# A layernorm, RWKV and mixture-of-experts kernel: raw x into the shared expert, zero copies behind the scatters, and another order of the work

## The chip, the cores and the metric

The kernel runs on one core of a Trainium2 chip. A core has five engines that run side by side, each through its own list of instructions in order: TensorE (PE, matmuls and transposes), VectorE (DVE), ScalarE (ACT), GpSimd (POOL) and SyncE (SP, which here only issues transfers). The metric is the device time of one execution in microseconds, and lower is better.

## The reference

x is 4 x 1024 tokens of 256 channels. The output is x + s * silu(f), where xn is the layernorm of x without weights, and s and f are two branches over xn:

```
xn = (x - mean(x)) / sqrt(var(x) + 1e-5)

s:  xt = layernorm(xn) * ln_w + ln_b ; prev = xt of the token before (0 at the first)
    K = (xt*mk + prev*(1-mk)) @ Wk.T ; V and R likewise ; R = sigmoid(R)
    S_t = S_(t-1) * decay + K_t      (a scan over the 1024 tokens of a sequence)
    s = xn + (R * ((S*first + K) * V)) @ Wo.T

f:  scores = sigmoid(xn @ router.T)      (8 experts in 2 groups of 4)
    the better group, then the top 2 experts of it, by scores + bias ; weights normed over the 2
    routed = sum over the 2 experts of weight * (silu(xn @ Wg) * (xn @ Wu)) @ Wd
    f = routed + (silu(xn @ sg) * (xn @ su)) @ sd    (the shared expert, for every token)
```

Each expert maps 256 to 128 channels and back. Everything is in float32.

## The kernel before

The 4096 tokens are 8 groups g of 512 (4 tiles of 128 tokens), and two routing batches b of 4 groups each. All of x stays in SBUF, with two more columns per token for its two routing weights. The work is cut into units, small functions, and a list written out by hand, ORDER (L25), calls them one by one. TensorE, VectorE and ScalarE run exactly in this order. The transfers that SP issues and the instructions of POOL that the list speaks of are chained too (`follow`), so that these two queues also go in the order of the list.

For a group: `moments` takes mean and variance of each tile (bn_stats, bn_aggr on VectorE), `root` and `invert` make rstd from them (ScalarE and VectorE), and `scale` (L369 to L373) writes (x - mean) * rstd over x, on VectorE or POOL as its last argument says. `turn_xn` transposes the scaled tiles to channels by tokens. `shared_in` (L869) multiplies them with one weight tile that holds the shared gate, the shared up, the router and a column of ones, so that one product per tile gives the shared expert's two halves, the router's logits and the sum over channels. `shared_turn` transposes the product of gate and up for the second half, which `shared_out` does much later. `norm2` makes rstd and offset of the second layernorm, `norm2_out` applies them on ScalarE (its result is xt), `turn_xt` transposes that. `mix` makes the three token shifted mixes, `gate`, `recur` and `value` do the products with Wr, Wk and Wv and the scan, `project_out` that with Wo.

For a routing batch: `choose`, `pick` (twice), `rank_pairs` and `place` are a chain of small operations on VectorE, with two matmuls in place, that ends in idx, a row for each token in a DRAM buffer xs. The two experts of a token make one of 19 pairs, and every pair has a region of its own in xs. `weigh` writes the two weights into the two further columns of x. `send` scatters the tokens into xs: 16 indirect transfers a batch, issued by POOL (L577), with an idle memset behind every other one (L587). `plan` and `slots` lay 128-token tiles over the filled regions.

Tiles are worked off in twos, u = 0 to 17: 4 pairs of tiles after the first batch, from whole tiles of its tokens, and 14 after the second. `tile_load` reads the rows from xs (SP, L729) once the batch's scatters have landed. `tile_turn` transposes, `tile_in` multiplies with gate and up of the two experts (the expert numbers come into registers of TensorE first), `tile_back` transposes, and `tile_out` multiplies with down, and SP writes the result to ys. After the second batch, the last tile of each of the 19 regions may end in rows that nothing was written to. So `slots` (1) also issues 19 transfers on SP (L672, "xs<-none") that put zeros behind the filled rows of each region, and the tiles of the last stage wait for them as well as for the scatters. `backs` finds where a token's result lies, `fetch` gathers it (POOL), `shared_out` and `final` add and multiply, `store` adds x and writes the output; for the last group `ready` and `finish` do the same in another order, with four writes of 128 tokens issued by SP. `over` handles inputs whose tiles are more than the 18 pairs; it isn't taken here.

`hold` is 6 transposes of a constant into a spare PSUM tile; there are 12 of them, before the first real work and around it. Transposed tiles go through 2 PSUM buffers (ps_tr), products through 4 (ps_mm), results of the down products through 2 (ps_dn).

Of the kernel before, what the change touches and what calls it, by code (L numbers as in the profile page):

```python
# [25 lines left out]
    ("moments", 0, 0), ("moments", 0, 1), ("moments", 0, 2), ("hold", 7, 6), ("moments", 0, 3), ("root", 0, 0, 1),  # L26
    ("hold", 9, 6), ("root", 0, 1, 2), ("root", 0, 2, 3), ("load_x", 4), ("hold", 8, 6), ("invert", 0, 0, 1),
    ("root", 0, 3, 4), ("invert", 0, 2, 3), ("invert", 0, 1, 2), ("invert", 0, 3, 4), ("scale", 0, 0, 0),
    ("load_x", 5), ("scale", 0, 3, 0), ("load_x", 6), ("scale", 0, 2, 0), ("scale", 0, 1, 0), ("hold", 4, 6),
    ("moments", 1, 0), ("hold", 3, 6), ("hold", 1, 6), ("hold", 10, 6), ("moments", 1, 1), ("moments", 1, 2),  # L30
    ("moments", 1, 3), ("root", 1, 0, 4), ("hold", 2, 6), ("moments", 2, 0), ("turn_xn", 0, 0), ("invert", 1, 0, 4),
    ("moments", 2, 1), ("moments", 3, 0), ("scale", 1, 0, 0), ("scale", 1, 2, 0), ("turn_xn", 0, 1), ("rates",),
    ("scale", 1, 1, 0), ("hold", 6, 6), ("hold", 11, 6), ("hold", 0, 6), ("moments", 2, 2), ("moments", 2, 3),
    ("moments", 3, 1), ("hold", 5, 6), ("root", 2, 0, 4), ("moments", 3, 2), ("moments", 3, 3), ("invert", 2, 0, 4),
    ("load_x", 7), ("root", 3, 0, 4), ("invert", 3, 0, 4), ("scale", 1, 3, 1), ("scale", 3, 1, 0),
    ("scale", 2, 0, 0), ("scale", 3, 0, 0), ("scale", 3, 2, 0), ("turn_xn", 1, 0), ("scale", 2, 3, 0),
    ("scale", 2, 1, 0), ("turn_xn", 1, 1), ("final_load", 0, 0), ("shared_in", 0, 0), ("moments", 4, 0),
    ("shared_in", 0, 1), ("moments", 4, 1), ("scale", 3, 3, 1), ("scale", 2, 2, 1), ("turn_xn", 3, 0),
    ("moments", 4, 2), ("moments", 4, 3), ("turn_xn", 3, 1), ("shared_in", 1, 0), ("moments", 6, 0),
    ("moments", 6, 1), ("moments", 6, 2), ("shared_turn", 0), ("shared_in", 1, 1), ("turn_xn", 2, 0), ("blank",),  # L40
    ("turn_xn", 2, 1), ("moments", 7, 0), ("moments", 7, 1), ("final_load", 1, 1), ("moments", 7, 2),
    ("moments", 7, 3), ("shared_in", 3, 0), ("root", 4, 0, 4), ("moments", 6, 3), ("root", 7, 0, 4),
    ("root", 6, 0, 4), ("norm2", 0, 2), ("invert", 4, 0, 4), ("invert", 7, 0, 4), ("scale", 4, 1, 0),
    ("moments", 5, 0), ("shared_in", 3, 1), ("shared_turn", 1), ("scale", 4, 2, 1), ("scale", 7, 3, 0),
    ("scale", 4, 0, 1), ("scale", 7, 2, 0), ("scale", 4, 3, 1), ("moments", 5, 1), ("load_experts",),
    ("invert", 6, 0, 4), ("shared_in", 2, 0), ("moments", 5, 2), ("load_squares",), ("scale", 6, 3, 1),
    ("shared_in", 2, 1), ("moments", 5, 3), ("scale", 6, 1, 1), ("choose", 0), ("scale", 6, 0, 1),
    ("turn_xn", 4, 0), ("turn_xn", 4, 1), ("root", 5, 0, 4), ("shared_turn", 2), ("scale", 6, 2, 1),
    ("norm2", 2, 2), ("pick", 0, 0), ("pick", 0, 1), ("shared_turn", 3), ("shared_in", 4, 0), ("turn_xn", 6, 0),
    ("turn_xn", 6, 1), ("weigh", 0), ("shared_in", 4, 1), ("scale", 7, 1, 1), ("scale", 7, 0, 1),  # L50
    ("invert", 5, 0, 4), ("turn_xn", 7, 0), ("turn_xn", 7, 1), ("rank_pairs", 0), ("norm2_out", 0),
    ("shared_in", 6, 0), ("scale", 5, 1, 1), ("shared_turn", 4), ("shared_in", 7, 0), ("norm2_out", 1),
    ("place", 0), ("turn_xt", 0, 0), ("scale", 5, 0, 0), ("plan", 0), ("scale", 5, 3, 1), ("shared_in", 6, 1),
    ("turn_xt", 0, 1), ("mix", 0, 2), ("scale", 5, 2, 1), ("turn_xn", 5, 0), ("shared_in", 7, 1), ("turn_xn", 5, 1),
    ("mix", 0, 0), ("mix", 0, 1), ("gate", 0), ("send", 0, 0), ("shared_turn", 6), ("turn_xt", 1, 0),
    ("recur", 0, 0), ("recur", 0, 1), ("turn_xt", 1, 1), ("slots", 0), ("send", 0, 1), ("shared_in", 5, 0),
    ("send", 0, 2), ("mix", 1, 2), ("shared_in", 5, 1), ("value", 0, 0, 0), ("choose", 1), ("send", 0, 3),
    ("shared_turn", 7), ("shared_turn", 5), ("norm2_out", 2), ("tile_load", 0), ("value", 0, 1, 0), ("pick", 1, 0),
    ("tile_load", 1), ("pick", 1, 1), ("gate", 1), ("turn_xt", 2, 0), ("turn_xt", 2, 1), ("tile_load", 2),
    ("tile_load", 3), ("rank_pairs", 1), ("project_out", 0, 1), ("project_out", 0, 0), ("tile_turn", 0),  # L60
    ("norm2_out", 3), ("place", 1), ("weigh", 1), ("tile_turn", 1), ("tile_in", 0, 0), ("tile_in", 0, 1),
    ("tile_turn", 2), ("plan", 1), ("mix", 1, 0), ("tile_in", 1, 0), ("send", 1, 0), ("send", 1, 1),
    ("tile_in", 1, 1), ("tile_back", 0), ("tile_in", 2, 0), ("tile_turn", 3), ("slots", 1), ("tile_in", 2, 1),
    ("mix", 1, 1), ("tile_back", 1), ("send", 1, 2), ("mix", 2, 2), ("send", 1, 3), ("tile_out", 0),
    ("turn_xt", 3, 0), ("tile_in", 3, 0), ("turn_xt", 3, 1), ("tile_in", 3, 1), ("mix", 2, 0), ("tile_back", 2),
    ("tile_load", 4), ("tile_load", 5), ("tile_out", 1), ("norm2", 4, 2), ("tile_back", 3), ("recur", 1, 0),
    ("norm2_out", 4), ("value", 1, 0, 1), ("tile_load", 6), ("recur", 1, 1), ("value", 1, 1, 0), ("mix", 2, 1),
    ("gate", 2), ("turn_xt", 4, 0), ("turn_xt", 4, 1), ("tile_load", 7), ("tile_out", 2), ("tile_turn", 4),
    ("tile_out", 3), ("norm2", 6, 2), ("tile_turn", 5), ("tile_in", 4, 0), ("tile_in", 4, 1), ("tile_turn", 6),
    ("backs", 0), ("tile_in", 5, 0), ("tile_back", 4), ("tile_in", 5, 1), ("norm2_out", 5), ("tile_load", 8),  # L70
    ("tile_turn", 7), ("tile_in", 6, 0), ("tile_back", 5), ("tile_in", 6, 1), ("tile_load", 9), ("tile_turn", 8),
    ("tile_out", 4), ("tile_back", 6), ("mix", 3, 0), ("tile_in", 7, 0), ("tile_in", 7, 1), ("backs", 1),
    ("mix", 3, 2), ("tile_load", 10), ("tile_turn", 9), ("tile_out", 5), ("tile_back", 7), ("tile_load", 11),
    ("tile_in", 8, 0), ("tile_in", 8, 1), ("tile_turn", 10), ("tile_out", 6), ("tile_back", 8), ("tile_in", 9, 0),
    ("tile_in", 9, 1), ("tile_turn", 11), ("tile_load", 12), ("tile_out", 7), ("tile_back", 9), ("tile_in", 10, 0),
    ("tile_in", 10, 1), ("tile_turn", 12), ("tile_load", 13), ("tile_load", 14), ("tile_out", 8), ("tile_back", 10),
    ("tile_in", 11, 0), ("tile_in", 11, 1), ("tile_turn", 13), ("tile_out", 9), ("tile_back", 11),
    ("tile_in", 12, 0), ("tile_in", 12, 1), ("tile_load", 15), ("tile_turn", 14), ("tile_out", 10),
    ("tile_load", 16), ("tile_back", 12), ("tile_in", 13, 0), ("tile_in", 13, 1), ("tile_load", 17),
    ("tile_turn", 15), ("tile_out", 11), ("tile_back", 13), ("recur", 2, 0), ("recur", 2, 1), ("norm2_out", 6),  # L80
    ("mix", 3, 1), ("turn_xt", 5, 0), ("turn_xt", 5, 1), ("tile_in", 14, 0), ("tile_in", 14, 1), ("tile_out", 12),
    ("tile_turn", 16), ("tile_in", 15, 0), ("tile_back", 14), ("tile_in", 15, 1), ("tile_turn", 17),
    ("tile_out", 13), ("tile_back", 15), ("tile_in", 16, 0), ("tile_in", 16, 1), ("tile_out", 14),
    ("tile_back", 16), ("tile_in", 17, 0), ("tile_in", 17, 1), ("tile_out", 15), ("tile_back", 17),
    ("tile_out", 16), ("tile_out", 17), ("project_out", 1, 1), ("value", 2, 1, 0), ("norm2_out", 7),
    ("value", 2, 0, 0), ("mix", 4, 2), ("project_out", 1, 0), ("recur", 3, 0), ("recur", 3, 1), ("fetch", 0, 0),
    ("shared_out", 0, 0), ("mix", 4, 0), ("fetch", 1, 0), ("shared_out", 1, 0), ("final", 0, 0), ("gate", 3),
    ("mix", 4, 1), ("fetch", 1, 1), ("fetch", 0, 1), ("turn_xt", 6, 0), ("turn_xt", 6, 1), ("shared_out", 0, 1),
    ("shared_out", 1, 1), ("value", 3, 0, 0), ("final", 1, 1), ("fetch", 2, 0), ("store", 0, 0, 1), ("final", 1, 0),
    ("final_load", 1, 0), ("shared_out", 2, 0), ("store", 1, 1, 1), ("project_out", 2, 0), ("value", 3, 1, 0),  # L90
# [24 lines left out]
def rwkv_times_moe_kernel(  # L115
# [46 lines left out]
    K = 2  # L162
# [896 lines left out]
```

## Time and profile before

| | |
|---|---|
| median of 7 runs | 315.74 us (314.74 to 317.28) |
| the profiled execution | 315.27 us, of which its span 313.5 us |
| busy TensorE, VectorE, ScalarE, POOL | 297.8, 213.7, 164.9, 123.5 us |
| first scatter of batch 0 issued | 52.27 us |
| last scatter of batch 0 issued | 75.73 us |
| first expert matmul of tile 0 | 84.20 us |
| scatters of batch 1 issued | 87.24 to 109.52 us |
| zero copies issued | from 96.7, the last at 110.7 us |
| last matmul starts | 307.3 us |

Times in the profile are us from the start of the span. A busy TensorE isn't TensorE at its peak, since matmuls overlap in the pipeline and their ends are modelled; where a price is wanted, the distance from one matmul's start to the next is the better measure. A group's line gives the line of the code, the engine, the operation, what it writes and reads, its count, then busy time and mean duration, then the idle time of the engine ahead of it and who ended that. "PEclk" is the clock that TensorE was granted. Idle time of an engine that isn't the bound costs nothing by itself.

### The profile page before, as it was taken

How to read it: one execution, taken by the hardware profiler on the slowest of the kernel's cores; microseconds unless marked ns; L12 is line 12 of the kernel's file. 1: busy time of each engine (PE TensorE's matmuls, PEld its weight loads, DVE VectorE, ACT ScalarE, POOL GpSimd, SP SyncE). 2: the span in 40 equal slices, each digit the busy share in tenths (PEclk: the TensorE clock that was granted, in tenths of full speed). 3: DMA queues.
4: the chain of work that ended last, by engine and by line, in shares of the span. 5: the costliest groups of instructions: out<-in, count | busy, mean ns of one | idle time of the engine just before them, and what ended most of it. 6: DMA issues, size and time to landing. Idle time of an engine off the chain costs nothing.

```text
span 313.5 us, 4693 instructions
## 1 busy us (share of the span) xinstructions
PE 297.8 (95%) x1334; PEld 221.7 (71%) x1334; DVE 213.7 (68%) x574; ACT 164.9 (53%) x342; POOL 123.5 (39%) x166
## 2 busy tenths in 40 slices
PE   7899879999799999999999999999999999999992
PEld 7887658576588658888888878885566656565551
DVE  4988899689896670848122162116999869899983
ACT  3688887866558867664334455334445233642200
POOL 7131928887078830000000000005735766395440
PEclk9999999999999999999999999999999999999997
DMA  6999820222515966132342310122335463454333
GB/s 194 346 377 339 248 95 18 84 84 86 137 67 154 266 173 204 44 94 69 98 105 67 101 37 33 67 69 81 94 95 158 142 202 86 149 154 113 104 104 106
DMA packets 37214, 41.10 MB, mean 131 GB/s; under 512 B 4016, under 2 KB 34736, under 8 KB 36880
## 3 DMA queue, kind: packets, MB, share of 16 engines
q1 hardware_dynamic: 33408, 31.92, 34.1%
q0 software_dynamic: 3216, 8.82, 8.8%
q8 instruction: 12, 0.20, 0.3%
q14 instruction: 18, 0.15, 0.2%
q10 hardware_dynamic: 560, 0.02, 0.1%
HBM read 24.46 MB, written 18.80 MB: 138 GB/s over the span
## 4 chain that ended last, share of the span: by engine, by line
PE 53%; DVE 19%; POOL 10%; DMA 7%; issue 5%; ACT 4%; SPq 1%; DVEq 0%; POOLq 0%
PE gu L753 20%; PE ye L779 10%; POOL xs L577 5%; PE v L812 4%; PE k L812 4%; DVE mix L804 4%; PE y L858 3%; PE trh L770 3%; PE tre L743 3%; DMA got<-ys,back 2%; PE r L812 2%; PE sh L876 2%; POOL got L907 2%; DMA xf<-in_x 2%; DVE S L834 1%
## 5 line engine op out<-in xcount | busy, mean ns | idle before, releaser
L907 POOL DMA_INDIRECT got<-ys,back x32 | 32.6, 1019 | 113.6 <-DMA ys<-yes 102.2
L753 PE MATMUL gu<-wgu,xeT 128*128 x288 | 66.5, 382 | 1.4 <-issue 1.3
L753 PEld LDWEIGHTS gu<-wgu,xeT 128*128 128x128 f32 x288 | 53.0, 190 | 8.7 <-issue 2.5
L761 DVE SCALAR_TENSOR_TENSOR act<-act,xe,gu 128x128 f32<-128x128 f32 x72 | 21.3, 343 | 47.3 <-ACT act L759 47.3
L802 ACT ACTIVATE mix<-xtT,vec 128x512 f32<-128x512 f32 x48 | 31.8, 718 | 23.6 <-PE k L812 15.7
L804 DVE SCALAR_TENSOR_TENSOR mix<-xtT,keep_of,mix 128x512 f32<-128x512 f32 x48 | 37.9, 835 | 4.9 <-ACT mix L802 4.6
L577 POOL DMA_INDIRECT xs<-xn,idx x32 | 32.9, 1029 | 18.3 <-DVE xn L571 10.0
L779 PE MATMUL ye<-wd,hT 128*128 x144 | 33.9, 380 | 0.0
L876 PE MATMUL sh<-wgus,xnT 128*128 128x265 f32 x128 | 31.2, 390 | 1.1 <-DVE hs L880 1.1
L759 ACT ACTIVATE act<-gu 128x256 f32<-128x256 f32 x36 | 13.6, 384 | 33.3 <-PE gu L753 23.5
L812 PE MATMUL v<-mix,wv 128*128 128x512 f32 x64 | 29.8, 593 | 0.0
L812 PE MATMUL k<-mix,wk 128*128 128x512 f32 x64 | 29.4, 593 | 0.0
L373 POOL TENSOR_SCALAR xn<-xn,mv,rstd 128x256 f32<-128x256 f32 x15 | 19.4, 1301 | 25.1 <-DVE rstd L368 25.1
L812 PE MATMUL r<-mix,wr 128*128 128x512 f32 x64 | 29.0, 596 | 0.0
L779 PEld LDWEIGHTS ye<-wd,hT 128*128 128x128 f32 x144 | 26.3, 191 | 3.0
L876 PEld LDWEIGHTS sh<-wgus,xnT 128*128 128x128 f32 x128 | 23.4, 191 | 5.5 <-DVE hs L880 2.0
L858 PE MATMUL y<-wo,A 128*128 128x256 f32 x112 | 26.1, 380 | 0.2 <-POOL A L439 0.2
L858 PEld LDWEIGHTS y<-wo,A 128*128 128x128 f32 x112 | 21.2, 190 | 5.9 <-issue 2.6
L812 PEld LDWEIGHTS r<-mix,wr 128*128 128x128 f32 x64 | 12.0, 190 | 13.9 <-issue 11.9
L812 PEld LDWEIGHTS k<-mix,wk 128*128 128x128 f32 x64 | 12.0, 191 | 11.7 <-issue 11.5
L820 ACT ACTIVATE rs<-r 128x512 f32<-128x512 f32 x16 | 9.2, 596 | 20.6 <-POOL A L439 9.1
L812 PEld LDWEIGHTS v<-mix,wv 128*128 128x128 f32 x64 | 12.1, 190 | 10.6 <-issue 9.8
(177 smaller groups left out, 480.2 us busy)
## 6 DMA issues: line engine op xcount, KB each, us to landing
xe<-xs SPq DMA_DIRECT2D x36, 129.0 KB, 2.2
ys<-yes SPq DMA_DIRECT2D x18, 256.0 KB, 2.1
xf<-in_x SPq DMA_DIRECT2D x16, 256.0 KB, 3.2
xn<-in_x SPq DMA_DIRECT2D x7, 512.0 KB, 7.0
out<-got SPq DMA_DIRECT2D x14, 256.0 KB, 2.3
ys<-zeros SPq DMA_DIRECT2D x1, 2816.0 KB, 14.0
xs<-none SPq DMA_DIRECT2D x19, 129.0 KB, 4.7
wgu<-in_w_gate SPq DMA_DIRECT2D x8, 128.0 KB, 3.3
```

What stands on the lines that cost most here:

```text
L373: scaled = (nc.gpsimd if eng else nc.vector).tensor_scalar(xn, xn, state[g]["mv"][:, n, 0:1], state[g]["rstd"][:, n : n + 1], ALU.subtract ...
L577: put = nc.gpsimd.indirect_dma_start(out=xs[:, :], out_offset=bass.IndirectOffsetOnAxis(ap=idx[:, n : n + 1], axis=0), in_=xn[:, n % NT, : ...
L753: nc.tensor.matmul(gu[:, k, :], p["xeT"][:, c, j, :], wgu[:, e, c, :], start=(c == 0), stop=(c == CC - 1))
L759: nc.scalar.activation(act, gu[:, :, 0:I], AF.Silu)
L761: nc.vector.scalar_tensor_tensor(act[:, k, :], act[:, k, :], p["xe"][:, j, C + k : C + k + 1], gu[:, k, I:], ALU.mult, ALU.mult)
L779: nc.tensor.matmul(y[:, j, :], p["hT"][:, j, k, :], wd[:, e, :], start=(k == 0), stop=(k == K - 1))
L802: nc.scalar.activation(m[:, c, :], xtT[:, c, 1 : G + 1], AF.Identity, scale=vec[:, c, which : which + 1])
L804: nc.vector.scalar_tensor_tensor(m[:, c, :], xtT[:, c, 0:G], keep_of[:, c, which : which + 1], m[:, c, :], ALU.mult, ALU.add)
L812: nc.tensor.matmul(ps, w[:, c, ts(dc, P)], src[:, c, :], start=(c == 0), stop=(c == CC - 1))
L858: nc.tensor.matmul(ps[:, j, :], A[:, c, ts(2 * h + j, P)], wo[:, c, :], start=(c == 0), stop=(c == CC - 1))
L876: nc.tensor.matmul(ps, st["xnT"][:, c, ts(n, P)], wgu_s[:, c, :], start=(c == 0), stop=(c == CC - 1))
L907: get = follow(nc.gpsimd.indirect_dma_start(out=got[:, j, :], out_offset=None, in_=ys[:, :], in_offset=bass.IndirectOffsetOnAxis(ap=route_ ...
```

## The change

It has six parts.

1. A new unit `center` multiplies the weight tile of the shared expert and router with ones, and takes the column means from it (two VectorE operations). `turn_xn` then transposes x as it was loaded, and `shared_in` puts rstd on its results: as the scale of the two ScalarE operations, and in a scalar_tensor_tensor in place of the product on VectorE. The column of ones goes. The weight tile is loaded by ScalarE's queue at the beginning instead of POOL's. `scale` is still there for every tile, since scatters and the second branch use xn, but it now stands behind the transposes; 25 of the 32 are on POOL and 7 on VectorE (15 and 17 before).
2. `norm2` takes the mean of xn as 0: it makes rstd alone, for both groups at once. `norm2_out` has no offset.
3. The zero copies are a unit of their own, `fills`, and the first of them waits until all scatters of batch 1 have landed.
4. Transposes of several tiles write them in reversed order (for raw x, group 0 excepted).
5. `finish` issues its output transfers on ScalarE's queue, and the halves of the last group are finished in the order 0, 1.
6. ORDER is another list throughout. `weigh` 0 stands behind `place` 0. `gate` 1, `turn_xt` 2 and `project_out` 0 stand behind the first tile's products and not ahead of them. `recur` 2, `value` 2, `project_out` 1, `mix` 3 and the first half of `recur` 3 stand ahead of `tile_turn` 4 and not far behind it. `rates` stands behind `gate` 0. Three `hold`s stand around `pick` 0 and `rank_pairs` 0.

```diff
+    wgu_s = wts.tile([P, CC, 2 * I + E], F32, tag="wgus", name="wgus")
+    nc.scalar.dma_start(wgu_s[:, :, 0:I], sw_gate.rearrange("(c p) i -> p c i", p=P))
+    nc.scalar.dma_start(wgu_s[:, :, I : 2 * I], sw_up.rearrange("(c p) i -> p c i", p=P))
...
+    def center():
+        ps = ps_mm.tile([P, 2 * I + E], F32, tag="mm", name="colsum")
+        for c in range(CC):
+            nc.tensor.matmul(ps, ones, wgu_s[:, c, :], start=(c == 0), stop=(c == CC - 1))
+        for c in range(CC):
+            nc.vector.scalar_tensor_tensor(wgu_s[:, c, :], ps, -1.0 / C, wgu_s[:, c, :], ALU.mult, ALU.add)
...
-        mean, var, rstd, off = st("mean"), st("var"), st("rstd2", 4), st("off", 4)
-        nc.vector.tensor_scalar(mean, raw_of[b][:, part, E], 1.0 / C, None, ALU.mult)
-        for i in range(many):
-            v, r = var[:, ts(i, NT)], state[g + i]["rstd"]
-            tt(v, state[g + i]["mv"][:, :, 1], r, ALU.mult)
-            tt(v, v, r, ALU.mult)
-        tt(off, mean, mean, ALU.mult)
-        tt(var, var, off, ALU.subtract)
+        var, rstd, r = st("var"), st("rstd2", 4), rstd_of[b][:, part]
+        tt(var, mv_of[b][:, part, 1], r, ALU.mult)
+        tt(var, var, r, ALU.mult)
         nc.scalar.activation(rstd, var, AF.Sqrt, bias=eps_t)
         nc.vector.reciprocal(rstd, rstd)
-        nc.vector.scalar_tensor_tensor(off, mean, -1.0, rstd, ALU.mult, ALU.mult)
...
+    def fills():
...
                 written.setdefault("fills", []).append(z.ins.name)
+                if first:
+                    after(z, f"puts{NB - 1}")
+                    first = False
                 follow(z, loose=True)
...
-            nc.scalar.activation(h, ps[:, 0:I], AF.Silu)
-            nc.scalar.copy(raw_of[b][:, hb * NT + n, :], ps[:, 2 * I :])
-            tt(h, h, ps[:, I : 2 * I], ALU.mult)
+            nc.scalar.activation(h, ps[:, 0:I], AF.Silu, scale=r)
+            nc.scalar.activation(raw_of[b][:, hb * NT + n, :], ps[:, 2 * I :], AF.Identity, scale=r)
+            nc.vector.scalar_tensor_tensor(h, ps[:, I : 2 * I], r, h, ALU.mult, ALU.mult)
...
-            follow(nc.sync.dma_start(out[b, hb * G + n * P : hb * G + (n + 1) * P, :], o[:, j, :]))
+            nc.scalar.dma_start(out[b, hb * G + n * P : hb * G + (n + 1) * P, :], o[:, j, :])
```

The two lists around the first tile, units on VectorE's small chain and on TensorE alone:

```
before: ... turn_xn 0 (after scale 0) ... shared_in 0 ... choose 0, pick 0, weigh 0, rank_pairs 0, place 0,
        gate 0, send 0, recur 0, value 0, gate 1, turn_xt 2, project_out 0, tile_turn 0, tile_turn 1, tile_in 0
after:  ... turn_xn 0, center, shared_in 0 ... choose 0, pick 0, rank_pairs 0, place 0, weigh 0,
        send 0, gate 0, recur 0, value 0, tile_turn 0, tile_turn 1, tile_in 0 ... project_out 0 ... gate 1
```

## The prediction

> **What bounds the kernel now.** I read the page first: busy shares, then the slices.
>
> ```profile
> PE 297.8 (95%) x1334; PEld 221.7 (71%) x1334; DVE 213.7 (68%) x574; ACT 164.9 (53%) x342; POOL 123.5 (39%) x166
> ...
> PE   7899879999799999999999999999999999999992
> ...
> DVE  4988899689896670848122162116999869899983
> ...
> PEclk9999999999999999999999999999999999999997
> ```
>
> TensorE is busy 95% of the span, at full clock in every slice but the last. Its digits under 9 are slices 1, 2, 5, 6, 11 and the last (one slice is 7.84 us): so a change can win only before about 90 us and in the tail. VectorE is at 8 and 9 for most of the first 13 slices, and again from 220 us. Next I read the chain of waits from 33 to 86 us (start, duration, what):
>
> ```profile
> 34.99 0.32 ACT sc L450
> 35.33 0.30 DVE choice L456
> ...
> 51.80 0.19 DVE idx L544
> 51.99 0.28 issue
> 52.27 1.09 POOL xs L577
> ...
> 75.73 2.53 DMA xs<-xn,idx
> 78.44 0.36 SPq L729
> 79.00 2.01 DMA xe<-xs
> 81.06 0.55 PE tre L743 x3
> ...
> 83.06 1.13 issue
> 84.20 1.99 PE gu L753 x8
> ```
>
> It runs from VectorE's routing (choose, pick, rank_pairs, place) to the first scatter at 52.27, through 16 scatters, which POOL issues one after the other, to the last at 75.73, its landing, the load of the first tile, and its first expert matmul (gu) at 84.20. From the first scatter to the first gu: 84.20 - 52.27 = 31.9 us. Call these S and T; T = S + 31.9. TensorE's waits after 14 us say how well the rest is covered; this one stands just ahead of tile 0:
>
> ```profile
> PE tre L743 <- DMA xe<-xs: 0.5, 1, 0.5
> PE trn L405 <- ACT hsT L887: 0.4, 1, 0.4
> ```
>
> Before, the first tile comes 0.5 us after TensorE has run out of other work: supply and demand meet. From 90 us to the end its waits are 0.3, 0.2, 0.2 and 0.2, some 1 us in all.
>
> **The change, part by part.**
>
> *Scales off VectorE, ahead of S.* VectorE up to idx, by form:
>
> ```profile
> L361 DVE BATCH_NORM_STATS2 st<-xn 128x6 f32<-128x256 f32 x32 | 13.0, 406 | 4.0 <-DMA xn<-in_x 4.0
> L373 DVE TENSOR_SCALAR xn<-xn,mv,rstd 128x256 f32<-128x256 f32 x17 | 6.7, 447 | 0.0
> ...
> L880 DVE TENSOR_TENSOR hs<-hs,sh 128x128 f32<-128x128 f32 x24 | 5.7, 276 | 0.4 <-issue 0.2 <-ACT raw L879 0.2
> ```
>
> In the new order no VectorE scale stands ahead of place 0: 17 at 0.39 (6.7/17) are 6.7 us less. Shared_in runs for 18 tiles ahead of place 0, not 24; its product becomes a scalar_tensor_tensor. That form takes 21.3/72 = 0.30 in the expert tiles (L761, same shape), so 18 x 0.30 = 5.3 against 24 x 0.24 = 5.7: nothing. Norm2 loses its mean and offset: from 37.48 to 39.52 it took 2.0 us, of which some 0.6 to 0.8 goes, twice: -1.4. Weigh 0 stood ahead of rank_pairs (43.59 to 46.35, 2.8 us); now it stands behind place, but scatters still need its columns in xn, of group 0 first, so 2.4 of it lies between idx and S: no gain. Center adds two VectorE passes over 128x264 from PSUM, between 0.34 (the 128x128 form above) and 0.68 (y L862, 128x512) each: +0.9. That is -7.2 us. I do not take it all, since choose waits for shared_in of four groups: in the new order TensorE does some 20 us of it (16 tiles of the shared expert at 0.9, eight xn transposes at 0.44, turns) from 13.4 us on, and ScalarE must then load the sigmoid table (1.28) and run sc (0.32): choose at about 32.5 rather than 35.3, 2.8 us earlier. From choose to idx it took 16.7 us; take off weigh 2.8, one norm2 1.9 and 1 to 2 of hs and inversions: 11 us, idx at 43.8, S at 43.8 + 2.4 + 0.3 = 46.5, or 5.8 us earlier than 52.27. Bounds: 44 (all 7.2, with 1 more for the chain) and 49 (POOL late: it has 18 scales ahead of the first send at 1.25 to 1.30, 23 us, from about 12.5 us on with waits for the third group's root: done at 36 at best, about 41 likely, 47 if it also waits for the later groups). The 13.4 (14.83 before): transposes no longer wait for scales, but the shared expert waits for center, behind 12 pairs of bn_stats and bn_aggr (12 x 0.59 = 7.1 on 4.0 of waits for x, center 0.9, a us for inversions and the later x).
>
> The new T is 46.5 + 31.9 = 78.4. The 16 scatters still go at 24.4/16 = 1.5 each; that POOL's leftover scales stand behind and between sends of batch 1 costs batch 0 nothing.
>
> *The new order: less work ahead of tile 0.* Units that stood ahead of the first tile's gu and now stand behind: gate 1 (8 matmuls of 512, 3.43), turn_xt 2 (two of 0.44) and project_out 0 (16 of 256, at 0.216 from start to start: 3.46), in all 7.8 us of TensorE work, with the VectorE and ScalarE work that goes with it. Behind tile 0 TensorE is dense in both. So the end moves by T's change plus 7.8: -5.8 + 7.8 = **+2.0 us**. Break-even: T 7.8 earlier, S at 44.5. The center's 4 matmuls (0.9) are before T, in the gap, free. So TensorE idles: it ran out of work at about 80.1 (80.6 less the 0.5 waited), now 7.8 + 1.4 earlier, at 70.9; tile 0's tre, at 81.06 in the chain, comes at 75.2. That is 4.3 us.
>
> *That idle stretch and the clock.* No idle of TensorE in the trace between 14 and 307 us is over 1.5 us. The one long idle is behind its last matmul at 307.3; windows (busy PE, PEld, DVE, ACT, POOL; PEclk; DMA):
>
> ```profile
> 307.30:309.30 2.00, 0.03 (x1) 0.00 (x0) 1.35 (x4) 0.00 (x0) 0.00 (x0) 1.00 0.76 255
> 309.30:311.30 2.00, 0.00 (x0) 0.00 (x0) 0.00 (x0) 0.00 (x0) 0.00 (x0) 0.63 0.29 90
> 311.30:313.50 2.20, 0.00 (x0) 0.00 (x0) 0.00 (x0) 0.00 (x0) 0.00 (x0) 0.50 0.02 4
> ```
>
> 0.63 over 2 us means half clock from about 309.8: it fell 2.5 us after the last matmul. An idle of 4.3 us reaches that. The trace shows no return to full clock, so the price is bounded by nothing (it stays, or returns at once) and by a half clock for as long as the idle was, 4.3 x 0.5 = 2.2 us. I take 1.0, the middle, since neither row is nearer.
>
> [...]
>
> *Fills behind the scatters.*
>
> ```profile
> L672 SPq DMA_DIRECT2D xs<-none x19: 497/502/638, 96.7 to 110.7; - x19
> ```
>
> Before, 19 fills were issued between 96.7 and 111.2 (14.5 us) beside batch 1's scatters, which were last issued at 109.5. Now the first waits for all 16 to land. With S of batch 1 at about 86 (87.2 before; plan, place and weigh 1 stand behind the same tiles) and 24 us of issuing, the last lands at about 110 to 111 (landings took 4 to 5 us beside fills, 2.5 to 3 without); fills issue until 125, land at 128.5; tile_load 4, behind them on SP, at 128.6, lands at 131. TensorE reaches tre 4 at about 132 (T 78.4 + 53.8 us of work ordered between; recur 2, value 2, project_out 1, half of recur 3 were put there). Margin 1 us: priced at nothing, its cover being that attention work; each us that batch 1 is late beyond it costs one. Queued on SP behind the waiting fill are tile_load 4 to 7 and the writes of yes 2 and 3; the latter have time until the fetches, some 100 us later. The other bound: fills 4 us late, +3.
>
> *The tail.* Finish's four out transfers leave SP's queue for ScalarE's, which is idle there: before, VectorE's last add began at 308.29 and the span ended 313.5; one issue of 0.3 us might be spared, at the other bound ScalarE's queue costs as much. Rates' two tables (2 x 1.28) now load behind gate 0, on a ScalarE that is 60% busy there: beside the scatters. Attention moved forward out of the tail leaves VectorE there less full; TensorE's waits there sum to 1 us, so at most that: -0.3. Reversed transposes: same count, nothing; at most 0.1 us a wait either way.
>
> Sum: +2.0 + 1.0 + 0 - 0.3 = +2.7 on the profiled 315.27 (span 313.5 and 1.8 around it): 318.0. That execution lies 0.5 below the median, 315.74; against the median: **318.4**.
>
> **The rivals.**
> A, faster: the routing chain is shorter than I think and S falls below 44.5. The place is VectorE between choose and the first send; the price is 1 us a us, and idle under 2.5 us leaves the clock alone. TensorE runs out of work at about 71, which bounds the gain at S = 42.2: -10.1 + 7.8 = -2.3, with 1 in the tail -3.3: 312.4 to 314.8. For: VectorE was 39.6 of 45 us busy up to 50, and 7.2 us of it go. Against: choose hangs on TensorE and ScalarE.
> B, slower still: the fills. If batch 1's scatters land after 112, tile 4 stalls TensorE, and a stall over 2.5 us halves the clock: +2 to +4 over my sum, 320 to 322.
> C, nothing: S is 1 to 1.5 us better than I say and the clock holds: 315 to 316.5. Also the case if TensorE's work is all that counts: it is nearly the same, 281 us by pitches, in both.
>
> **How the numbers follow.** What this kernel's runs can tell from no change is 0.3%, 0.95 us: 314.8 to 316.7. Mine (316.7 to 319.8) 0.42; B 0.17; C 0.11, of which a part spills; A 0.30. Range: from A's middle, 313, to B's far half, 321.5, leaves 1 in 10 at each end. Faster 0.30, same 0.10, slower 0.60.
>
> **What the profile after would show.** Right: no scale on VectorE ahead of idx; first scatter at 45 to 48; TensorE idle of 3 to 5 us ahead of the first tre, PEclk under 1 in the slice behind it; gu at 77 to 80; fills from 110 to 125; tre 4 without wait; last y some 2 to 3 us later. Wrong, if the first scatter comes ahead of 44.5, if work fills the stretch before tile 0, or if tre 4 waits for xe.

## The result, and the profile after

The changed kernel takes 318.68 us (median of 18 runs, 318.01 to 319.89) against 315.74 (46 runs, 314.44 to 318.06): a ratio of 1.0095, 95% interval 1.0082 to 1.0109. It is slower by 2.9 us, and the forecast was 318.4. Some executions are slower at a lower granted clock (the kernel before on one of the experiments' chips: 321.7 to 324.9 us at 0.987 to 0.990, beside 314.8 to 319.3 at 0.995 to 0.999); every profiled execution shown here is a fast one. That of after has a span of 316.2 us, against 313.5. The page of after, the same four lines:

```profile
PE 298.3 (94%) x1338; PEld 223.0 (71%) x1338; DVE 211.3 (67%) x541; ACT 164.4 (52%) x339; POOL 135.9 (43%) x174
...
PE   7999978897899999999999999999999999999991
...
DVE  2779887989996895952212711321489999889973
...
PEclk9999999999999999999999999999999999999999
```

VectorE is 2.4 us less busy and POOL 12.4 us more: the scales went over. TensorE does as much as before, and its slices under 9 are still the last and some of the first eleven. The seventh and eighth, at 8, and the tenth (71.1 to 79.1 us), at 7, are new among them; the tenth is the stretch ahead of tile 0. The chain of waits up to the first tile (start, duration, what):

```profile
34.06 0.32 ACT sc L453
34.41 0.38 DVE choice L459
...
75.36 0.66 DVE A L851
76.02 1.14 DVE S L846
...
79.18 0.40 DVE row L542
79.58 0.66 issue
80.24 3.69 PE gu L764 x16
```

choose starts at 34.41 instead of 35.33, the first gu at 80.24 instead of 84.20. The scatters are no longer the named chain, since several waits end close together here. The step that the chain names last, VectorE's row, is not what holds gu: in finish_on_sp below, gu starts at 80.99 us and this row only at 81.72. POOL's timeline has the first of them (in brackets what POOL waited for):

```profile
48.88 1.08 POOL L580 DMA_INDIRECT xs<-xn,idx  x1 [5.22 <-DVE hs L893]
```

It goes at 48.88, 3.4 us earlier than before. TensorE's waits between 12 and 90 us:

```profile
PE pos L539 <- DVE pair L521: 2.0, 1, 2.0
PE tre L754 <- DMA xe<-xs: 2.0, 2, 1.8
PE gu L764 <- DVE row L542: 1.0, 1, 1.0
```

The wait ahead of tile 0 is 2.0 us, where it was 0.5: supply now comes after demand. VectorE's groups up to the first scatter, the two that answer to those of before:

```profile
L372 DVE BATCH_NORM_STATS2 st<-xn 128x6 f32<-128x256 f32 x32 | 12.9, 405 | 6.8 <-DMA xn<-in_x 6.8
L893 DVE SCALAR_TENSOR_TENSOR hs<-sh,rstd,hs 128x128 f32<-128x128 f32 x20 | 6.3, 341 | 1.2 <-ACT raw L892 0.9
```

No scale is among them any more (6.7 us before). But the idle time ahead of bn_stats, for x, went from 4.0 to 6.8 us. With the scales gone, VectorE comes to the tiles of x earlier and waits for them: it did 7 scales (2.5 us) in its first 14 us before and does none now, and it is done with the first 12 tiles at 13.7 us before and at 13.8 after. The zero copies:

```profile
L680 SPq DMA_DIRECT2D xs<-none x19: 497/501/648, 104.7 to 118.6; - x19
```

They begin at 104.7 us. The last scatter of batch 1 is issued at 111.8. So they are later than before (96.7), but they do not wait for the scatters: the wait that the change writes down isn't in force.

**Where the 2.7 us of span come from.** For the sum I count TensorE's work as each of its records at the median distance from start to start of its kind (gu 0.216 us, r 0.429, transposes 0.109). Then the end of the last matmul is the first gu, plus the work behind it, plus the waits behind it (all that is left over; time lost to half clock is in it).

| us | first scatter | TensorE out of work | first tre | first gu | work behind | waits behind | last matmul ends | span |
|---|---|---|---|---|---|---|---|---|
| before | 52.3 | 80.0 | 80.7 | 84.2 | 219.5 | 3.5 | 307.2 | 313.5 |
| after | 48.9 | 74.8 | 76.7 | 80.2 | 227.2 | 2.1 | 309.5 | 316.2 |

The first gu comes 4.0 us earlier, 7.7 us more work stands behind it, 1.4 us of waits are gone: +2.3. The rest, 0.4, lies behind the last addition (4.8 us to the end of the span before, 5.2 after).

### The profile page after: what moved, and what is told of

It is laid out like the page before. It is cut to its first block, busy times and chain, and to the rows that moved or that the text cites. A ratio compares the mean times of both kernels' runs of the same rounds, so it can differ in the third digit from the quotient of the medians.

```text
span 316.2 us, 4706 instructions
## 1 busy us (share of the span) xinstructions
PE 298.3 (94%) x1338; PEld 223.0 (71%) x1338; DVE 211.3 (67%) x541; ACT 164.4 (52%) x339; POOL 135.9 (43%) x174
## 4 chain that ended last, share of the span: by engine, by line
PE 78%; DVE 11%; ACT 4%; DMA 3%; issue 2%; ACTq 0%; DVEq 0%
PE gu L764 20%; PE ye L791 10%; PE y L870 8%; PE k L824 8%; PE r L824 8%; PE v L824 8%; PE sh L889 6%; PE dn L931 4%; PE trh L782 2%; PE tre L754 2%; PE trt L410 2%; DMA xn<-in_x 2%; DMA wgus<-in_sw_up 1%; ACT L453 1%; DVE S L846 1%
## 5 line engine op out<-in xcount | busy, mean ns | idle before, releaser
L580 POOL DMA_INDIRECT xs<-xn,idx x32 | 34.1, 1066 | 15.6 <-issue 10.1
L814 ACT ACTIVATE mix<-xtT,vec 128x512 f32<-128x512 f32 x48 | 31.9, 714 | 13.0 <-PE k L824 12.6
L384 POOL TENSOR_SCALAR xn<-xn,mv,rstd 128x256 f32<-128x256 f32 x25 | 31.6, 1278 | 13.0 <-PE hold L1013 6.7
L816 DVE SCALAR_TENSOR_TENSOR mix<-xtT,keep_of,mix 128x512 f32<-128x512 f32 x48 | 34.8, 767 | 3.5 <-ACT mix L814 3.5
L770 ACT ACTIVATE act<-gu 128x256 f32<-128x256 f32 x36 | 13.8, 384 | 35.9 <-PE gu L764 26.6
L889 PE MATMUL sh<-wgus,xnT 128*128 128x264 f32 x128 | 30.9, 389 | 1.2 <-DVE hs L893 1.0
L793 ACT COPY yes<-ye 128x512 f32<-128x512 f32 x18 | 10.5, 585 | 16.9 <-PE ye L791 15.8
```

The lines of the kernel that those rows point to most:

```text
L384: scaled = (nc.gpsimd if eng else nc.vector).tensor_scalar(xn, xn, state[g]["mv"][:, n, 0:1], state[g]["rstd"][:, n : n + 1], ALU.subtract ...
L580: put = nc.gpsimd.indirect_dma_start(out=xs[:, :], out_offset=bass.IndirectOffsetOnAxis(ap=idx[:, n : n + 1], axis=0), in_=xn[:, n % NT, : ...
L770: nc.scalar.activation(act, gu[:, :, 0:I], AF.Silu)
L814: nc.scalar.activation(m[:, c, :], xtT[:, c, 1 : G + 1], AF.Identity, scale=vec[:, c, which : which + 1])
L816: nc.vector.scalar_tensor_tensor(m[:, c, :], xtT[:, c, 0:G], keep_of[:, c, which : which + 1], m[:, c, :], ALU.mult, ALU.add)
L889: nc.tensor.matmul(ps, st["xnT"][:, c, ts(n, P)], wgu_s[:, c, :], start=(c == 0), stop=(c == CC - 1))
```

## The experiments

They ran on three chips on which the runs of the kernel before alone lay between 314.8 and 328.2 us, against 314.4 to 318.1 in the comparison above. So the medians are given, but what is compared are places in the profiled executions, as in the table. Its rows for all of them:

| us | first scatter | TensorE out of work | first tre | first gu | work behind | waits behind | last matmul ends |
|---|---|---|---|---|---|---|---|
| before_filler_late | 52.0 | 76.3 | 80.6 | 84.3 | 222.9 | 4.4 | 311.7 |
| after_filler_late | 48.5 | 70.9 | 76.2 | 80.3 | 230.6 | 7.5 | 318.5 |
| filler_small | 49.0 | 75.9 | 77.0 | 80.5 | 226.3 | 4.9 | 311.7 |
| filler_back | 49.7 | 91.5 | 91.5 | 94.4 | 219.4 | 11.2 | 325.0 |
| fills_wait | 49.3 | 75.2 | 77.3 | 80.9 | 227.2 | 3.7 | 311.7 |
| weights_behind_x1 | 51.3 | 78.7 | 79.1 | 82.8 | 227.2 | 5.1 | 315.0 |
| no_mid_holds | 49.0 | 75.0 | 77.2 | 80.8 | 227.2 | 5.5 | 313.6 |
| finish_on_sp | 49.3 | 76.3 | 77.2 | 81.0 | 227.2 | 4.2 | 312.4 |
| after_code_before_order | 64.7 | 86.9 | 92.1 | 96.2 | 219.5 | 6.7 | 322.3 |
| raw_x_old_order | 55.9 | 87.7 | 87.7 | 92.0 | 219.5 | 4.9 | 316.3 |
| after_no_memset | 48.5 | 86.9 | 86.9 | 90.2 | 227.2 | 12.4 | 329.7 |
| before_no_memset | 51.8 | 86.4 | 86.4 | 89.4 | 219.5 | 17.6 | 326.5 |

Kernels whose order behind tile 0 is that of after (fills_wait, weights_behind_x1, no_mid_holds, finish_on_sp) have 3.7 to 5.5 us of waits there on these chips, against 2.1 in after's own profile. finish_on_sp differs from after in the last four transfers alone and already has 4.2, so differences in that column of a us or two are not put down to an edit.

One column follows another through the whole table. In the ten kernels, before and after included, in which TensorE runs out of work ahead of the first tre, the first gu comes 31.3 to 32.3 us after the first scatter, whether that goes at 48.5 or at 64.7 us. In the other four TensorE still has work when tile 0 could start, and gu comes 36 to 45 us after it.

### Filler moved behind tile 0, in the kernel before

```diff
-    ("tile_load", 3), ("rank_pairs", 1), ("project_out", 0, 1), ("project_out", 0, 0), ("tile_turn", 0),
+    ("tile_load", 3), ("rank_pairs", 1), ("tile_turn", 0),
...
-    ("norm2_out", 3), ("place", 1), ("weigh", 1), ("tile_turn", 1), ("tile_in", 0, 0), ("tile_in", 0, 1),
+    ("norm2_out", 3), ("place", 1), ("weigh", 1), ("tile_turn", 1), ("tile_in", 0, 0), ("tile_in", 0, 1),
+    ("project_out", 0, 1), ("project_out", 0, 0),
```

> The kernel before with project_out 0 (3.46 us of TensorE work) moved from ahead of tile 0 to behind its products; nothing else. Theory (the end is the first gu plus the TensorE work behind it): first scatter and first gu stay at 52.3 and 84.2 us, TensorE idles some 4 us ahead of the first tre instead of 0.5, and the run is 3.2 to 3.5 us longer, 319.0 to 319.3. If the idle stretch also halves TensorE's clock, as the idle behind the last matmul did after 2.5 us: 1 to 2 us more, 320 to 321, with a PEclk under 1.00 in the windows behind it. Rival (TensorE's total work is all that counts, where it stands does not matter): 315.7.

Measured: 319.87 us in the profiled execution (median 322.74). TensorE's waits between 70 and 90 us, and the windows around the first tile (busy PE, PEld, DVE, ACT, POOL; PEclk; DMA):

```profile
PE tre L743 <- DMA xe<-xs: 4.1, 1, 4.1
```

```profile
78.00:80.00 2.00, 0.00 (x0) 0.00 (x0) 1.90 (x8) 0.00 (x0) 0.00 (x0) 1.00 0.30 68
80.00:82.00 2.00, 1.43 (x5) 1.20 (x6) 0.31 (x1) 0.07 (x1) 0.00 (x0) 0.64 0.92 247
82.00:84.00 2.00, 2.00 (x6) 1.21 (x6) 0.05 (x1) 2.00 (x5) 0.00 (x0) 0.51 0.76 210
84.00:88.00 4.00, 4.00 (x21) 3.54 (x20) 3.68 (x13) 2.73 (x4) 0.00 (x0) 1.00 0.02 6
```

The first gu stands still (84.3 for 84.2), the work behind it grows by 3.4 and the last matmul ends 4.5 us later (1 us of it in waits further on). So TensorE's total isn't what counts: work that moves from ahead of tile 0 to behind it is paid in full. The granted clock did fall, to half (0.64 and 0.51 in the two windows from 80 to 84 us), and was back by 84 us. Yet the first gu was hardly late (32.3 us after the first scatter for 31.9): the half-speed work ahead of gu took the place of the 1.1 us that TensorE waited there in before; here it had no wait but the 4.1.

### The same in the kernel after

```diff
-    ("value", 0, 1, 1), ("scale", 5, 3, 1), ("tile_load", 1), ("value", 0, 0, 1), ("tile_turn", 0),
+    ("scale", 5, 3, 1), ("tile_load", 1), ("tile_turn", 0),
...
     ("tile_load", 2), ("tile_in", 0, 1),
+    ("value", 0, 1, 1), ("value", 0, 0, 1),
```

> The kernel after with value 0 (3.43 us of TensorE work) moved from ahead of tile 0 to behind its products: the suspected cost, doubled. Theory: the wait ahead of the first tre grows from 1.9 to some 5.3 us, the first gu stays at 80.2, the run is 3.4 us longer than after, 322.1. If the clock falls in the idle stretch: 323 to 324. Rival (only total work counts): 318.7.

Measured: 326.44 us (median 327.29). Up to tile 0 it went as expected: the wait ahead of tre is 5.2 us, the first gu at 80.3, the clock at half from about 74.5 to 81.3 (0.50 granted in the windows from 75 to 81), again hardly making gu late (its first 0.9 us ran at half clock), and 3.4 us more work behind it. The run is 4 us longer than that, mostly by one wait of 3.1 us at 247.6 us and half clock after it (0.74, 0.50 and 0.91 granted in the windows of 2 us from 251): TensorE waited for an addition of VectorE, and that for 2.2 us on something that the profile doesn't name. The edit doesn't explain it. Up to tile 0 it supports the theory; the total is inconclusive.

### Filler put back, much and little

```diff
-    ("value", 0, 1, 1), ("scale", 5, 3, 1), ("tile_load", 1), ("value", 0, 0, 1), ("tile_turn", 0),
+    ("value", 0, 1, 0), ("scale", 5, 3, 1), ("tile_load", 1), ("value", 0, 0, 0), ("norm2_out", 2), ("turn_xt", 2, 0),
+    ("turn_xt", 2, 1), ("mix", 1, 2), ("gate", 1), ("project_out", 0, 1), ("project_out", 0, 0), ("tile_turn", 0),
```

> The kernel after with gate 1, turn_xt 2 and project_out 0 (7.8 us of TensorE work, with norm2_out 2 and one mix) back ahead of tile 0, as in the kernel before; value 0's last product on VectorE as there. Theory: what TensorE waited there (1.9, 0.4 and 1.0 us) is filled, the first gu is at about 85, and the run is 1.5 to 2.9 us shorter than after, 315.8 to 317.2. If VectorE, which is full between 64 and 79 us, can't take the added mix and xn in time, half of that. Rival (only total work counts): 318.7.

Measured: 333.48 us (median 333.65). My expectation missed by far. TensorE's waits between 60 and 90 us:

```profile
PE r L824 <- DVE mix L816: 3.8, 1, 3.8
PE trt L410 <- ACT xt L422: 1.6, 1, 1.6
```

gate 1 waited for VectorE's mix and turn_xt 2 for ScalarE, the clock fell (its 8 matmuls took 6.0 us for 3.4; granted over the whole run were 0.976, in after 0.998), and tile 0, whose rows had long landed, stood behind it all: first gu at 94.4. In the order of after, this much filler cannot simply be put back: what it needs from VectorE and ScalarE comes too late there. That it is the routing of batch 1 that keeps VectorE from it was not tested.

```diff
-    ("scale", 4, 0, 1), ("norm2_out", 3), ("recur", 0, 0),
+    ("scale", 4, 0, 1), ("norm2_out", 2), ("recur", 0, 0),
...
-    ("value", 0, 0, 1), ("tile_turn", 0),
+    ("value", 0, 0, 1), ("turn_xt", 2, 0), ("turn_xt", 2, 1), ("tile_turn", 0),
```

> The kernel after with turn_xt 2 alone (0.87 us of TensorE work, two ScalarE evictions) ahead of tile 0, and norm2_out 2 changed places with norm2_out 3. TensorE waits 1.9 us there, and this work needs almost nothing from VectorE. Theory: the first gu stays at 80.2, TensorE's wait falls by 0.9, the run is 0.9 us shorter than after, 317.8. Rival (only total work counts): 318.7. If ScalarE is late with xt 2: tre comes later and the run is 318.7 to 319.5.

Measured: 319.78 us (median 321.30). The wait ahead of tre falls from 2.0 to 1.1 and the work behind gu by 0.9, as expected; the last matmul ends 0.7 us earlier than in finish_on_sp and 1.9 earlier than in no_mid_holds, which ran on the same chip. That is the direction and about the size, but no more than the chip's scatter.

### Zero copies that really wait

`apart` declares that writers of xs don't wait for each other. The edit takes the first zero copy out of this.

```diff
-                apart(z, "xs")
+                if not first:
+                    apart(z, "xs")
```

> The kernel after with the first zero copy left out of the declaration that says that writers of xs don't wait for each other. In after the first zero copy was issued at 104.7 us and the last scatter at 111.8, so that the wait that the change writes down is not in force there; here it should be. Theory (the zero copies are off the path while they land before TensorE comes to the first tile of the last stage, at about 134): zero copies from 115 to 129, tile_load 4 at 133 and landed at 135, TensorE waits 0 to 3 us for tre 4, run 318.7 to 321.5. Rival (the place of the zero copies does not matter): 318.7.

Measured: 320.48 us (median 320.91). The zero copies:

```profile
L680 SPq DMA_DIRECT2D xs<-none x19: 496/502/1075, 113.8 to 129.2; - x19
```

They now wait for the last scatter (issued at 111.2), so it was this declaration that had taken the wait away. tile_load 4 goes at 132.05 and lands at 134.75. TensorE starts tre 4 at 134.83, without a wait, against 134.12 in after; the 0.7 us are those by which its first gu is late. So even copies that wait in earnest cost TensorE nothing at tile 4: the attention work ahead of it covers them, with 0.1 us to spare.

### The weights behind x

```diff
-    nc.scalar.dma_start(wgu_s[:, :, 0:I], sw_gate.rearrange("(c p) i -> p c i", p=P))
-    nc.scalar.dma_start(wgu_s[:, :, I : 2 * I], sw_up.rearrange("(c p) i -> p c i", p=P))
...
+    load_x(1)
+    follow(nc.sync.dma_start(wgu_s[:, :, 0:I], sw_gate.rearrange("(c p) i -> p c i", p=P)))
+    follow(nc.sync.dma_start(wgu_s[:, :, I : 2 * I], sw_up.rearrange("(c p) i -> p c i", p=P)))
+    load_x(2)
+    load_x(3)
```

> The kernel after with the loads of the shared gate and up weights moved from the head of ScalarE's queue to SP's queue behind x of groups 0 and 1; nothing else. VectorE waited 6.8 us for x in its first 11 us in after and 4.0 in before. Theory (the early weight load took bandwidth from x and with it about 2 us from the chain to the first scatter): the waits for x fall to 4 to 5 us, the shared expert starts at 12.2 to 13.2 instead of 14.2, the first scatter goes at 47 to 48 instead of 48.9, the run is 1 to 2 us shorter than after, 316.7 to 317.7. Rival (the weights then come late for center, which holds the shared expert back): shared expert at 14 to 15, run 318.7 or more.

Measured: 323.47 us (median 322.23). The time is the rival's. VectorE's waits up to 16 us:

```profile
DVE st L373 <- DMA xn<-in_x: 7.2, 5, 3.0
```

The waits for x are no shorter, 7.2 us. Groups 0 and 1 came sooner, but VectorE then waited 2.0 us for group 2, and center stands behind group 2 in VectorE's order. So the rival's reason isn't shown: center's matmuls ran at 10.7 us (12.3 in after), and the weights were not late for it. TensorE idled 1.8 us, the clock fell to half from about 14.7 to 18.1 (0.68, 0.50 and 0.97 granted in the windows from 14, 16 and 18 us), and the first scatter went 2.5 us later.

What the early weights cost x stays open. The waits of before and after (4.0 and 6.8 us) overstate it, since VectorE now comes to x earlier. In before it came to group 2 at 10.34 us and found it there; in after it waited for it until 10.92. From 6 to 16 us the transfers run at some 270 to 370 GB/s in these kernels, and at that rate the 0.26 MB of weights would take 0.7 to 1.0 us, an estimate.

### The holds, and the finish

```diff
-    ("hold", 4, 6), ("hold", 6, 6),
...
-    ("hold", 11, 6),
```

> The kernel after without the three holds around pick 0 and rank_pairs 0 (18 transposes of a constant, 2 us of TensorE). Theory: they stand where TensorE waits for the routing chain anyway, and the first scatter decides; the first gu stays at 80 to 81, the run within 0.5 us of after, 318.2 to 319.2, and TensorE only waits longer there. If the longer wait halves the clock, half clock for some 3.5 us of the shared expert behind it, up to 1.8 us of that on the path if TensorE runs out later than tile 0 comes. Rival (a part of the predicted idle of 4.3 us was lost to these holds): TensorE runs out at 72.7 instead of 74.8 and the run doesn't change either.

Measured: 321.92 us (median 322.12). The first gu is at 80.8, and TensorE is out of work at 75.0, not at 72.7: the waits in the routing chain grew by what the holds had taken (pos: 2.8 us for 2.0; trn: 1.8 for 0.5). The holds filled waits; they weren't on the path. The clock fell twice here, to half for some 3.4 us each time: from 41.1 us (0.77, 0.50 and 0.87 in the windows from 40, 42 and 44 us), which didn't reach tile 0, and from 78.6 us, behind a wait of 2.0 us ahead of the first tre, about as long as the one that left it at full speed in after (1.00). In the windows from 78, 80 and 82 us it was 0.66, 0.50 and 0.99. The first gu still came 31.8 us after the first scatter, but its first 1.2 us ran at half clock, which is 0.6 us of work late.

```diff
-            nc.scalar.dma_start(out[b, hb * G + n * P : hb * G + (n + 1) * P, :], o[:, j, :])
+            follow(nc.sync.dma_start(out[b, hb * G + n * P : hb * G + (n + 1) * P, :], o[:, j, :]))
```

> The kernel after with the last four output transfers issued by SP again; nothing else. From the last VectorE addition's end to the span's end it took 4.8 us before and 5.15 in after. Theory: the 0.35 us come from ScalarE's queue; the tail goes back to 4.8, run 318.3. Rival (the order of the halves or chance): 5.15 stays, 318.7.

Measured: 321.10 us (median 321.78). From the last addition to the end of the span it took 5.4 us, more than with ScalarE's queue (5.2). Over all these kernels this tail lay between 4.7 and 5.4 us whichever queue issued. So the theory fell: ScalarE's queue isn't shown to cost anything. Two kernels with after's queue and after's order of the halves, filler_small and after_filler_late, have 4.7, so the 0.4 us of the tail are within what varies from run to run.

### The new code in the old order

The order of before, with center ahead of the first shared_in, each scale behind its group's transposes, and the scales of after's engines:

```diff
-    ("scale", 0, 3, 0), ("load_x", 6), ("scale", 0, 2, 0), ("scale", 0, 1, 0), ... ("turn_xn", 0, 1),
+    ("load_x", 6), ... ("turn_xn", 0, 1), ("scale", 0, 0, 1), ("scale", 0, 3, 1), ("scale", 0, 2, 1), ...
...
+    ("center",), ("shared_in", 0, 0),
```

> The code of after in the order of the kernel before: raw x into the transposes, center, reversed transposes, and the division of scale between POOL and VectorE as in after; each scale that stood ahead of its group's transposes now right behind them; weigh 0 ahead of rank_pairs as before. Theory: the shortened VectorE chain brings the first scatter to 49 to 50.5, TensorE has 7.8 us more to do than in after until the first tile and doesn't wait for it, first gu at 81 to 82.5, run 312.5 to 314. Rival (the new parts give nothing by themselves, and the early weight load takes from the load of x what the scales give back): first scatter at 51 to 52, run 315 to 316.

Measured: 330.77 us (median 332.54). POOL's timeline ahead of the first scatter:

```profile
46.63 5.18 POOL L384 TENSOR_SCALAR xn<-xn,mv,rstd 128x256 f32<-128x256 f32 x4 [1.78 <-PE trn L410]
62.87 1.65 POOL L384 TENSOR_SCALAR xn<-xn,mv,rstd 128x256 f32<-128x256 f32 x1 [11.05 <-PE trn L410]
64.69 1.08 POOL L580 DMA_INDIRECT xs<-xn,idx  x1 [0.17 <-issue]
```

With raw x a scale has to wait until the transposes have read its tile. In the old order a scale of batch 1, whose transposes come late, stands ahead of the first send in POOL's queue, and the scatters of batch 0 waited 11 us behind it. This cost is one that the parts alone don't show: raw x needs an order made for it. A second arrangement takes the late scales out of the way:

```diff
-    ("scale", 6, 3, 0), ("scale", 6, 1, 1), ("scale", 6, 0, 0), ("scale", 6, 2, 0), ...
-    ("scale", 7, 3, 1), ("scale", 7, 2, 1), ("scale", 7, 1, 1), ("scale", 7, 0, 1), ...
+    ("plan", 0), ("scale", 6, 3, 0), ("scale", 6, 2, 0), ("scale", 7, 3, 0), ("scale", 7, 2, 0), ("scale", 5, 0, 0),
...
-    ("scale", 5, 1, 0), ("scale", 5, 0, 0), ("scale", 5, 3, 1), ("scale", 5, 2, 0), ...
+    ("send", 0, 3), ("scale", 6, 1, 1), ("scale", 6, 0, 1), ("scale", 7, 1, 1), ("scale", 7, 0, 1), ("scale", 5, 1, 1),
```

> The code of after in the order of the kernel before, with the scales arranged so that POOL isn't late (in the earlier run of that kind the first scatter waited for POOL's 25 scales, until 64.7 us): groups 0, 1 and 3 all on POOL right behind their transposes, those of groups 5, 6 and 7 behind place 0 on VectorE or behind send 0 on POOL. Theory: VectorE's chain is some 3 us shorter, the first scatter goes at 48.5 to 50, but in this order TensorE has other work until about 80 to 81, so that tile 0 now waits for TensorE: the first gu at 82.5 to 84, run 314 to 316, hardly better than before. Rival (an earlier first scatter is worth its time): first gu at 80.5, run 312 to 312.5.

(Here one tile of group 5 is scaled ahead of its transposes, so its shared expert and logits aren't the reference's.) Measured: 324.72 us (median 325.26). Neither theory: the first scatter goes at 55.9, later than before, released by VectorE. choose starts at 38.45 there, 3.1 us later than before, after 7.1 us of waits for x (4.0 before) and 3.8 for ScalarE's evictions of the shared expert. So in these two arrangements the new code doesn't shorten the routing chain by itself; what gain there is in after came with the new order too.

### The idle memsets

```diff
-            if n % 2:
-                follow(nc.gpsimd.memset(idle, 0.0))
```

> The kernel after without the idle memset on POOL behind every other scatter (8 in a batch, 0.54 us and some 0.06 of issue each; the memset's result is used nowhere). Theory (the arrival of tile 0 sets the end, until TensorE runs out of other work, which it does at 74.8 us in after): the last scatter goes 3.6 to 4 us earlier, TensorE's wait ahead of the first tre (1.9 and 0.4 us) goes, first gu at 78, run 2.3 us shorter than after, 316.4. Rival (TensorE's total work is all that counts, or VectorE, which is full until 79 us, sets the first gu): 318.2 to 318.7.

> The kernel before without the same idle memsets. Theory: TensorE waits there only 0.5 and 0.3 us for tile 0, so the same 3.6 to 4 us on the scatters give 0.6 to 0.8: 315.0. Rival (a scatter chain that is shorter is worth its time wherever it stands): 312.

Measured: 337.97 us (median 337.63) and 334.99 (median 336.32). The scatters did go faster, the last at 68.0 us in after_no_memset, but both kernels became some 19 to 20 us slower (the last matmul ends at 329.7 for 309.5 us, and at 326.5 for 307.2), so this pair says nothing on the question it was made for. Windows of after_no_memset (columns as above):

```profile
62.00:64.00 2.00, 1.48 (x6) 0.94 (x6) 0.00 (x0) 0.00 (x0) 1.60 (x2) 1.00 0.19 66
64.00:66.00 2.00, 0.00 (x0) 0.00 (x0) 0.00 (x0) 0.59 (x1) 1.49 (x2) 1.00 0.32 114
66.00:68.00 2.00, 0.00 (x0) 0.00 (x0) 0.00 (x0) 0.00 (x0) 1.43 (x2) 0.76 0.24 85
```

While POOL issues scatter after scatter, TensorE stands still for 6.5 us, VectorE for 7.8 and ScalarE, with one instruction between, for 2.9 and 3.6. The profile names no event that ends it; the first of them, ScalarE, starts again at 69.00 us, when the last scatter's instruction ends (69.01). In after, with the memsets, TensorE is busy for 7.4 of the 8 us from 62 to 70, VectorE for 6.6 and ScalarE for 8.0.

## Why the prediction was right, and which of its terms were not

The mechanism was right in its main part: the work that moves behind tile 0 is paid in full, the earlier first scatter pays only what it brings tile 0 forward, and the first is more than the second. That the sum, +2.7 us of span, was met to 0.1 us is luck. The first gu gained 4.0 us and not 5.8, which is 1.8 more on the sum, and against that stand 1.0 for the clock and 0.7 in the waits and the tail that did not come as forecast. Of the signs named for the profile after, three came: no scale on VectorE ahead of idx, tre 4 without a wait, the last y 2.3 us later. The first scatter, the first gu (80.24 for 77 to 80), TensorE's idle time, the clock and the place of the fills lay outside what was named.

- *Filler*: right. 7.8 us was forecast to move behind tile 0; 7.7 did. before_filler_late shows that such work is paid in full while tile 0 stands still.
- *S at 46.5*: it was 48.9, so the gain is 3.4 us and not 5.8. From choose to idx it took the 11.0 us forecast. But choose began at 34.4, not 32.5. The forecast's own terms don't give 32.5: 13.4 + 20 + 1.28 + 0.32 is 35.0. In after TensorE has 17.4 us of work there, not 20, but the shared expert started at 14.2, not 13.4, since what the scales freed on VectorE went into waits for x (6.8 us), and a wait for VectorE's product behind a table load of ScalarE (1.28 us, from 23.9) stopped it for 0.6 at 25.6. And from the start of weigh to the first scatter it took 3.4 us, not 2.7: by the profile POOL was released by the product that stands behind all of weigh, not by the two columns of the first group.
- *T - S of 31.9*: 31.4, and 31.3 to 32.3 in every kernel in which TensorE waits for tile 0.
- *TensorE out of work at 70.9, idle 4.3*: at 74.8, idle 2.0. The waits between 14 and 63 us are longer than before (5.5 us for 3.8) and three holds stand among them; I had taken them as unchanged. no_mid_holds shows that the holds themselves don't matter. The 4.3 was also misread: the 81.06 of the chain is the later part of the first transposes, which began at 80.65.
- *The clock, +1.0*: nothing in after's profile, where an idle of 2.0 us did not bring it down (1.00 granted in every window from 72 to 88 us); in no_mid_holds an idle of the same length did (0.50 between 80 and 82). The runs with idles of 4.1 and 5.2 us show that half clock there makes the first gu late by half a us at most, as counted from the first scatter; where it lasts into gu, 0.5 to 0.6 us of gu's work is late (after_filler_late, no_mid_holds). The price of an idle stretch depended here on what ran behind it; I had charged it blind.
- *The tail and the waits behind tile 0, -0.3*: the waits fell by 1.4 us, and the tail gave 0.4 back. On the other chips such kernels have 3.7 to 5.5 us of waits, so the fall is not shown to come from the change.
- *Fills at nothing*: right in size, wrong in the mechanism. I had read the wait in the code as one in force; the first copy went 7 us ahead of the last scatter. fills_wait shows the forecast's own picture with the wait in force, some 3 to 4 us later than drawn: copies issued until 129 (forecast 125), tile_load 4 at 132.05 (128.6), landed at 134.75 (131), tre 4 at 134.83 (132). The margin was 0.1 us and not 1, but there was no wait, and rival B falls.

Rival A falls with S, which was 48.9 and not under 44.5. Its remark that an idle of under 2.5 us leaves the clock alone falls too: a wait of 2.1 us halved it in finish_on_sp (0.50 granted between 44 and 46 us). Rival C's reason, that TensorE's total work is all that counts, falls with before_filler_late.

## What to carry to other kernels

When an engine is full from some point on, the end is that point plus the work behind it: count for every unit on which side of it it stands, and charge moved work in full. A transfer chain that becomes shorter pays only as far back as the moment at which the other work is exhausted, and work put ahead of it pays only if the engines that feed this work can deliver (in filler_back TensorE waited 3.8 us for VectorE's mix); look for the filler's own suppliers before moving it. And read waits in a trace, not in the code: one written down here was not in force, and in these two kernels a memset that looked idle was worth some 19 us.

## What the runs showed of the hardware that was not expected

**The clock's fall didn't come at a fixed delay.** From the end of the last matmul it took 2.5 us in before (0.63 granted between 309.3 and 311.3) and some 5.2 us in after (0.77 granted between 313.5 and 316). The same wait of some 2 us ahead of the routing's first matmul (pos), in kernels that are equal up to there, left the clock at full speed in after and filler_small (1.00 in the windows from 40 to 48 us) and halved it in finish_on_sp. The windows of finish_on_sp:

```profile
40.00:42.00 2.00, 0.04 (x1) 0.07 (x1) 1.82 (x10) 1.45 (x3) 1.34 (x2) 1.00 0.89 296
42.00:44.00 2.00, 1.89 (x5) 1.07 (x6) 1.26 (x3) 0.82 (x4) 1.63 (x1) 0.74 0.76 261
44.00:46.00 2.00, 2.00 (x6) 1.58 (x5) 1.76 (x5) 0.10 (x1) 0.00 (x0) 0.50 0.00 1
46.00:48.00 2.00, 2.00 (x13) 1.73 (x12) 1.79 (x10) 1.32 (x5) 0.00 (x0) 0.91 0.00 0
```

Half clock for (0.26 x 2 + 0.50 x 2 + 0.09 x 2) / 0.5 = 3.4 us, so some 1.7 us of work late. A wait of some 2 us was enough to bring it down in some of these runs and not in others.

**Without the memsets between the scatters the other engines stood still.** 16 indirect transfers issued some 1.3 us apart (the first at 48.5, the last at 68.0 us in after_no_memset), without the memset in between, went with long stretches in which the other engines started nothing: 6.5 us on TensorE and 7.8 on VectorE in after_no_memset (62 to 70 us), and 8.6, 9.2 and 8.8 us on TensorE, VectorE and ScalarE in before_no_memset (104 to 117 us). What they wait for, the traces don't name; it stays open.
